# Layer 1 of a graph network: the table of ready halves written in steps of three chunks and read from the third gathered block on

## The chip, the core and the metric

The kernel runs on one core of one Trainium2 chip. The metric is the device time of one execution in microseconds (us); lower is better. The engines are named as in the profile: PE (TensorE, matrix products), DVE (VectorE), ACT (ScalarE), POOL (GpSimd, which issues the gathers) and SP (SyncE, which issues most other DMAs). PEld and SPq are PE's weight loads and SP's queue.

## What is computed

A graph network of three layers over 6250 nodes with 256 features and 100,000 edges that are sorted by destination, then a residual and a layer norm. Cut to what matters:

```python
loops = arange(n)
src, dst = concat([edges[0], loops]), concat([edges[1], loops])
deg = segment_sum(ones, dst);  dinv = rsqrt(deg)
h = x
for W, b in ((W1, b1), (W2, b2), (W3, b3)):      # 256->512, 512->512, 512->256
    msg = (h @ W)[src] * (dinv[src] * dinv[dst])[:, None]
    h = relu(segment_sum(msg, dst) + b)
out = layernorm(x + h)
```

The kernel sums over the edges before it multiplies by W1 (both are linear), so layer 1 sums rows of `dinv * x`, 256 numbers each.

## The kernel before

**Blocks and chunks.** The nodes are cut into 50 blocks of 125 (`NB`, `Q`). Each block has a run of 2048 places for edges, that is 16 chunks (`KF`) of 128 edges. Edges beyond these are gathered for ten blocks at once (`GRP`).

**Two ways to sum a block.** A *gathered* block takes its 16 chunks one after the other. POOL gathers the 128 source rows of a chunk by an indirect DMA (L1179), DVE makes one-hot matrices of the destinations (`shot`, L1130), and PE multiplies the one-hot matrix with the rows and adds up in a PSUM bank (L1209). A *dense* block instead uses a matrix of edge counts between its nodes and all nodes. Such counts are made on the chip (`counts`: one-hots of small windows of edges by DVE at L791, products at L866, copies out of PSUM by ACT at L825), stored to DRAM (`kept`, L818), converted by ACT (`piece`, L1139), and multiplied with `parts` (L1278).

**Halves.** `parts` holds `dinv * x` in SBUF, each row as a high half and a low half of 256 columns in the format fp32r. One product with 512 columns sums both halves. Layer 1 has three ways to get a gathered row:

- blocks before `BOTH_FROM` gather plain rows of 256 fp32 numbers from `tables[0]` (128 x 1 KB per chunk) into one of eight row buffers (`rows`). Their product is an fp32 matmul with 256 columns, which the trace records as two instructions of 256 columns. The block's own row (the self loop) is one more product with an identity matrix (L1192).
- blocks from `BOTH_FROM` to 47 gather rows of 512 ready halves from the DRAM table `both_halves` (in the profile `both`; 128 x 2 KB per chunk) into one of eleven buffers (`split`). Their product is one fp32r matmul with 512 columns. The block's own row is added by DVE (L1314) after the sum.
- blocks 48 and 49 (`TAIL_FROM`) gather plain rows and split them on ACT and DVE (L1241, L1244).

**The table of halves.** `both_stored` (L1499) writes `parts` to the table by ten stores of five blocks, 125 x 5 rows of 2 KB or 1.28 MB each. `by_rows` (L73) makes two DMAs of every store, of 112 and of 13 partitions. The generator yields 5 after each store: it continues five chunks later. A gather from the table names the whole table as its input, so the first one waits for all ten stores.

**The order of the work.** `layer` (L1048) writes all engines' queues out by hand, chunk by chunk. For layer 1 the gathered blocks are 22 to 49, so item 0 is the gather for the group of ten, items 1 to 16 are block 22, items 17 to 32 block 23, items 33 to 48 block 24, items 49 to 64 block 25 and items 65 to 80 block 26. In each chunk come the gather of that item, the product of the item five chunks back (`BOTH_LAG`), the steps that follow an ended block (`after1`: scaling, transposes at L1299, the product with W1 at L1335, the store of the result to `tab1`), then the fixed extras (`both_stored` starts at chunk 2; the counts and the searches for windows, which end in a gather at L521, start at 0), and at the end up to three dense products. Each engine works through its own queue in order; SP's queue holds the stores of the table, those of the counts (`kept<-room`) and those of the results (`tab<-st`). In the program's order the first two counted blocks are stored in chunks 18 and 31.

**A room that is lent.** When the first six chunks of block `BOTH_FROM` have been issued (L1164), a part of the row buffers becomes a third buffer for the one-hots of the counts (`late_hot_room`).

Of the kernel before, what the change touches and what calls it, by code (L numbers as in the profile page):

```python
# [47 lines left out]


FEW = 22  # L50
BOTH_FROM = 26
BOTH_LAG = 5
TAIL_FROM = 48
TAIL_LAG = 7
# [18 lines left out]
def by_rows(queue, tile_rows, dram_rows, store=False):  # L73

    for s in (slice(0, EVEN), slice(EVEN, Q)):
        if store:
            queue.dma_start(out=dram_rows[s], in_=tile_rows[s])  # L77
        else:
            queue.dma_start(out=tile_rows[s], in_=dram_rows[s])
# [320 lines left out]
def sorted_path(ctx: ExitStack, tc: tile.TileContext, x, edges, starts, found, wts, biases, room, late, out):  # L400
# [647 lines left out]
    def layer(i, width, gathered, dense, after, rows, first=0, spacing=1.0, extras=(), filler=None):  # L1048
# [53 lines left out]
        def sum_bank(name, most):  # L1102
            nonlocal late
            if i == 0:
                while not common:
                    if early_copy[0]():
                        break
                    late += 1
                    go(chunk)
                return common.popleft()  # L1110
            need(now, name, most)
            return idle[name].pop(0)
# [33 lines left out]
        def of_both(c):  # L1146

            n, b, _ = items[c]
            return i == 0 and (n * GRP >= BOTH_FROM if b is None else BOTH_FROM <= b < TAIL_FROM)

# [9 lines left out]
        def gather(c):  # L1160
            nonlocal turn
            n, b, j = items[c]
            table = both_halves if of_both(c) else tables[i]
            if (i, b, j) == (0, BOTH_FROM, BOTH_LAG + 1):  # L1164
                hot_stores.appendleft(late_hot_room)
# [16 lines left out]
        def product(c):  # L1182
# [4 lines left out]
            if j == 0:  # L1187
                acc = sum_bank("acc", 2 if i == 1 else 3)
                own_product = i == 0 and b < BOTH_FROM
                if own_product:  # L1190
# [113 lines left out]
    def after1(b, acc, bank):  # L1304
        got = []
        yield from take("zs", 2)
        zs = work.tile([Q, HID], F32, name="szs")
        if b < BOTH_FROM:
            nc.scalar.activation(zs[:, :C], acc[:Q, C:], AF.Copy, scale=dinv[:, b:b + 1])
# [189 lines left out]
    def both_stored(first):  # L1499

        for b in (*range(first, NB, GRP // 2), *range(0, first, GRP // 2)):
            to = slice(b, b + GRP // 2)
            by_rows(nc.sync, parts[:, to].bitcast(F32),
                    both_halves[b * Q:(b + GRP // 2) * Q, :].rearrange("(b p) c -> p b c", p=Q), store=True)
            yield 5

    def steps(b):

# [12 lines left out]
    first = 16  # L1521
    spacing = 15.0
    layer(0, C, every[FEW:], few, after1, first_rows, first, spacing, [(0, other_parts()), (2, both_stored(2 * GRP)), (0, searches), (1, counts(many[:FEW + EXTRA], places, GB, True)), (0, team_work)])

    assert len(common) == 7 - len(team_banks)
# [209 lines left out]
```

## Time and profile before

| | |
|---|---|
| three runs | 2097.81, 2102.70 and 2103.22 us; median 2102.7 |
| the profiled execution | 2106.41 us, its span 2104.7 us, mean granted PE clock 0.958 |
| PE, DVE, POOL, ACT busy, share of the span | 92%, 75%, 69%, 64% |
| gathers of layer 1 | from 78.8 us on; the first from the table of halves at 182.9 us |
| DMA over the span | 494.26 MB, mean 235 GB/s |

The profile gives, for one execution, each engine's busy time, its instructions in order of time, and for an idle stretch what released the engine. The window view gives busy time, the granted PE clock (1.00 is full speed), the mean busy share of the 16 DMA engines and their rate for chosen stretches. A line such as `L1209 PE MATMUL smm<-room,shot` is an instruction by its line of the kernel, its engine, and what it writes and reads. In a timeline the columns are start, duration, engine, line, operation, names, shapes, count, and in brackets the idle time before it with its releaser.

### The profile page before, as it was taken

Reading aid. Unit: us, or ns where it says so; the run is one execution under the profiler, and the core shown is the slowest. Engines: PE = TensorE matmul, PEld = TensorE weight load, DVE = VectorE, ACT = ScalarE, POOL = GpSimd, SP = SyncE. Lnnn points to the kernel's source line nnn. Section 1 sums busy time; section 2 is a strip of 40 time slices with the busy share of each in tenths; the row PEclk is TensorE's granted clock in tenths of the full one; section 3 lists DMA queues with packets and bytes.
Section 4 is the critical chain, followed back from the end, with each engine's and each line's share of the span. In section 5 each row is a group of like instructions: output and inputs, shape, how many; then the busy total and the mean of one; then the engine's idle time right before and its main releaser. Section 6 shows DMA issues by size and latency. Waiting matters only on the chain. (4 is left out here: it accounts for less than half of the span.)

```text
span 2104.7 us, 30190 instructions
## 1 busy us (share of the span) xinstructions
PE 1946.5 (92%) x8645; PEld 1507.4 (72%) x8645; DVE 1570.6 (75%) x2963; ACT 1351.5 (64%) x2587; POOL 1442.0 (69%) x1442
## 2 busy tenths in 40 slices
PE   3499999999997988999999999999898899999996
PEld 2377777777774656888778877888676777777774
DVE  5876777787777578777877778787776377777777
ACT  0566777677776666767766767777565455555553
POOL 2466766776767477767766777667776477777775
PEclk6599999999999989999999999999998899999998
DMA  7887989999999999899997999999988376767674
GB/s 156 260 250 222 255 241 246 245 265 252 255 261 308 240 274 263 255 260 286 279 262 209 294 273 275 258 267 271 252 231 240 91 190 176 188 178 189 177 185 117
DMA packets 236333, 494.26 MB, mean 235 GB/s; under 512 B 43807, under 2 KB 86889, under 8 KB 236155
## 3 DMA queue, kind: packets, MB, share of 16 engines
q0 software_dynamic: 122112, 311.41, 53.7%
q1 hardware_dynamic: 98203, 168.96, 29.2%
q10 hardware_dynamic: 15840, 11.86, 2.3%
q8 instruction: 70, 1.15, 0.2%
q14 instruction: 108, 0.88, 0.1%
HBM read 424.61 MB, written 67.46 MB: 234 GB/s over the span
## 5 line engine op out<-in xcount | busy, mean ns | idle before, releaser
L1179 POOL DMA_INDIRECT room<-tab,ssrc x1040 | 1077.8, 1036 | 394.6 <-issue 164.5
L1244 DVE TENSOR_TENSOR halves<-room,halves 128x512 fp32r<-128x512 f32 (+1 forms) x776 | 424.1, 561 | 226.2 <-ACT halves L1241 223.8
L1241 ACT CAST halves<-room 128x512 fp32r<-128x512 f32 (+1 forms) x776 | 386.3, 517 | 222.5 <-DMA room<-tab,ssrc 192.6
L1209 PE MATMUL sacc<-halves,shot 128*125 128x512 f32 x1401 | 494.6, 418 | 31.0 <-DVE halves L1244 16.4
L1179 POOL DMA_INDIRECT halves<-both,ssrc x352 | 331.5, 942 | 142.9 <-issue 36.3
L1209 PEld LDWEIGHTS sacc<-halves,shot 128*125 128x125 f32 x1401 | 261.8, 191 | 120.8 <-DVE halves L1244 35.8
L1139 ACT CAST piece<-room 125x625 fp32r<-125x625 uint8 x416 | 294.5, 716 | 75.3 <-DVE halves L1244 21.9
L791 DVE TENSOR_TENSOR room<-near_cols,slots 128x625 bf16<-128x625 f32 (+2 forms) x390 | 294.2, 802 | 42.6 <-PE sacc L866 17.7
L1130 DVE TENSOR_TENSOR shot<-near_cols,sdlo 128x500 fp32r<-128x500 f32 x371 | 247.7, 668 | 6.4 <-PE smm L1209 3.7
L1278 PE MATMUL mat_ps<-parts,piece 125*125 125x512 f32 x650 | 187.0, 405 | 0.0
L1244 DVE TENSOR_TENSOR parts<-room,parts 128x512 fp32r<-128x512 f32 x200 | 136.3, 692 | 58.6 <-ACT parts L1241 57.9
L1278 PE MATMUL win_ps<-parts,piece 125*125 125x512 f32 x600 | 171.2, 406 | 4.9 <-ACT piece L1139 4.8
L1278 PE MATMUL smm<-parts,piece 125*125 125x512 f32 x605 | 171.8, 402 | 0.6 <-DVE piece L1139 0.6
L1241 ACT CAST parts<-room 128x512 fp32r<-128x512 f32 x200 | 121.8, 622 | 64.3 <-DMA room<-tab,ssrc 57.4
L939 DVE TENSOR_TENSOR parts<-parts 125x512 fp32r<-125x512 f32 x200 | 137.9, 690 | 32.2 <-ACT parts L937 29.4
L977 PE MATMUL sacc<-parts 125*125 125x512 f32 x400 | 143.7, 434 | 17.6 <-ACT parts L937 9.7
L825 ACT CAST room<-sacc 125x500 uint8<-125x500 f32 (+1 forms) x152 | 105.6, 703 | 71.9 <-PE sacc L866 56.8
L866 PEld LDWEIGHTS <-room 128*125 128x125 bf16 x650 | 89.5, 140 | 76.6 <-issue 29.6
L1278 PE MATMUL sacc<-parts,piece 125*125 125x512 f32 x450 | 142.2, 423 | 0.4 <-ACT piece L1139 0.4
L977 PE MATMUL mat_ps<-parts 125*125 125x512 f32 x400 | 137.6, 425 | 0.7 <-DVE room L1378 0.7
L1278 PEld LDWEIGHTS mat_ps<-parts,piece 125*125 125x125 f32 x650 | 116.7, 187 | 27.8 <-issue 2.3
L1278 PEld LDWEIGHTS win_ps<-parts,piece 125*125 125x125 f32 x600 | 111.3, 189 | 33.3 <-ACT piece L1139 5.8
(345 smaller groups left out, 3252.6 us busy)
## 6 DMA issues: line engine op xcount, KB each, us to landing
parts<-tab SPq DMA_DIRECT2D x105, 448.0 KB
kept<-room SPq DMA_DIRECT2D x29, 683.6 KB
room<-kept SPq DMA_DIRECT2D x29, 683.6 KB
room<-tab,ssrc POOLq DMA_INDIRECT x1040, 5.6
tab<-st SPq DMA_DIRECT2D x62, 224.0 KB
both<-parts SPq DMA_DIRECT2D x10, 1120.0 KB
own_row<-tab SPq DMA_DIRECT2D x38, 224.0 KB
parts<-kept SPq DMA_DIRECT2D x60, 136.7 KB
```

Of the source, the lines that this page charges most:

```text
L791: nc.vector.tensor_tensor(out, near_cols[:, :shape[2]].unsqueeze(1).to_broadcast(shape), numbers.unsqueeze(2).to_broadcast(shape), op=ALU. ...
L825: nc.scalar.copy(place[:, :, u * G:(u + len(ms)) * G].rearrange("p k (t r) -> p t k r", r=G), counted_in.rearrange("p (t v) -> p t v", t=2 ...
L866: nc.tensor.matmul(bank[:Q, len(pair) * 256:][:, :G * NB], lhsT=hot_lo, rhs=hot_key, start=True, stop=True)
L939: nc.vector.tensor_sub(to[:, HID:], row, to[:, :HID].bitcast(F32))
L977: nc.tensor.matmul(team_banks[n][:Q], lhsT=team_pieces[(g * CUTS + k // PIECE) % 2][n][:, k % PIECE, :], rhs=both_parts[u % 3][:, h * HID: ...
L1130: nc.vector.tensor_tensor(hot[:, :n], near_cols[:, :Q].unsqueeze(1).to_broadcast([P, n, Q]), dlo.rearrange("p b j -> p (b j)")[:, at:at + ...
L1139: convert(piece, made_or_read[:, c * PIECE:(c + 1) * PIECE, :])
L1179: nc.gpsimd.indirect_dma_start(out=row, out_offset=None, in_=table, in_offset=bass.IndirectOffsetOnAxis(ap=at, axis=0))
L1209: nc.tensor.matmul(acc[:Q, :size], lhsT=hot, rhs=row[:, c0:c0 + size], start=(not own_product and k == c0 == 0), stop=(k == KF and c0 + si ...
L1241: nc.scalar.copy(halves[:, :width], landed[chunk - hi_lag])
L1244: nc.vector.tensor_sub(halves[:, width:], landed.pop(chunk - lo_lag), halves[:, :width].bitcast(F32))
L1278: nc.tensor.matmul(acc_d[:Q], lhsT=got[done // PIECE][:, k % PIECE, :], rhs=parts[:, k], start=(k == 0), stop=(k == NB - 1))
```

## The change

`both_stored` continues three chunks after each store, not five: the ten stores are issued in chunks 2, 5, 8, ..., 29, not 2, 7, 12, ..., 47. `BOTH_FROM` becomes 24, not 26: blocks 24 and 25 (items 33 to 64) gather ready halves from the table instead of plain rows, have no own product at L1192 and get their own row by L1314; the room for one-hots is lent at chunk 39, not 71.

```diff
 FEW = 22
-BOTH_FROM = 26
+BOTH_FROM = 24
 BOTH_LAG = 5
...
             by_rows(nc.sync, parts[:, to].bitcast(F32),
                     both_halves[b * Q:(b + GRP // 2) * Q, :].rearrange("(b p) c -> p b c", p=Q), store=True)
-            yield 5
+            yield 3
```

## Prediction

> **What bounds the kernel now.** I read the windows of layer 1's start first, then the timelines of PE, SP and POOL, the waits of PE, and the list of DMA issues. The span of the profiled execution is
>
> ```profile
> span 2104.7 us, 30190 instructions
> ```
>
> and its time 2106.41 us: 1.7 us lie around the span, and it is 3.7 us (0.18%) above the median of 2102.7 us. I work with differences in the profiled execution and carry them over to the median. About 0.3%, or 6.3 us, is what a measurement of this kernel can tell from no change.
>
> The windows (length, busy time of PE, PEld, DVE, ACT, POOL, granted clock, DMA share, rate):
>
> ```profile
> 78.00:84.00 6.00, 0.00 (x0) 0.00 (x0) 6.00 (x4) 1.95 (x1) 4.92 (x2) 0.50 0.47 131
> 84.00:102.00 18.00, 8.11 (x29) 6.05 (x30) 15.94 (x22) 3.94 (x7) 12.30 (x10) 0.54 1.00 310
> 102.00:114.00 12.00, 9.60 (x38) 7.07 (x37) 11.72 (x22) 5.80 (x9) 9.20 (x10) 0.72 0.55 170
> 114.00:138.00 24.00, 21.94 (x111) 17.05 (x110) 16.74 (x26) 17.51 (x30) 15.15 (x17) 1.00 0.81 245
> 138.00:162.00 24.00, 24.00 (x120) 18.71 (x119) 17.19 (x32) 17.15 (x31) 15.92 (x18) 1.00 0.98 311
> 162.00:180.00 18.00, 18.00 (x83) 13.18 (x81) 10.48 (x20) 10.31 (x20) 10.17 (x11) 1.00 0.51 163
> 180.00:200.00 20.00, 20.00 (x95) 14.91 (x94) 13.07 (x27) 12.24 (x21) 13.95 (x16) 1.00 0.85 227
> ```
>
> From 138 us on PE has no idle time at all, at full clock: there PE is the bound, and every matmul time that goes is gained. Before that, PE is idle for parts of the time. The DMA engines are full in two stretches (share 1.00 and 0.98), and both times they move 310 to 311 GB/s: I take 0.31 MB/us as what they can do with this mix. Between, from 102 to 138, they have room.
>
> SP's queue shows where the stores stand:
>
> ```profile
> 81.51 16.19 SPq L77 DMA_DIRECT2D both<-parts  x8
> 114.17 0.76 SPq L77 DMA_DIRECT2D kept<-room  x2
> 114.97 5.78 SPq L77 DMA_DIRECT2D both<-parts  x4
> 134.97 0.77 SPq L77 DMA_DIRECT2D kept<-room  x2
> 135.79 10.73 SPq L77 DMA_DIRECT2D both<-parts  x6
> ```
>
> Four stores (two DMAs each) are issued as fast as SP gets them through. Then SP stands at the store of the first counted block until its counts are ready at 114.17, passes two more stores, stands again until 134.97, and passes three more; the tenth comes after a third such store. So the schedule in chunks matters little by itself: what counts is on which side of a counted block a store stands.
>
> **The matmuls: what is gained.** One chunk on PE with plain rows, one with ready halves, and an own product:
>
> ```profile
> 133.71 0.60 PE L1209 MATMUL win_ps<-room,shot 128*125 128x256 f32 x2
> 134.14 0.38 PE L866 MATMUL sacc<-room 128*125 128x250 bf16 x2
> 134.28 0.95 PE L1278 MATMUL sacc<-parts,piece 125*125 125x512 f32 x3
> 135.06 0.60 PE L1209 MATMUL win_ps<-room,shot 128*125 128x256 f32 x2
> ```
>
> ```profile
> 199.52 0.39 PE L1209 MATMUL smm<-halves,shot 128*125 128x512 f32 x1
> 199.76 0.38 PE L866 MATMUL sacc<-room 128*125 128x250 bf16 x2
> 199.89 0.94 PE L1278 MATMUL sacc<-parts,piece 125*125 125x512 f32 x3
> 200.67 0.39 PE L1209 MATMUL smm<-halves,shot 128*125 128x512 f32 x1
> ```
>
> ```profile
> 144.44 0.39 PE L1192 MATMUL smm<-parts,ident_r 125*125 125x512 f32 x1
> 144.67 0.60 PE L1209 MATMUL smm<-room,shot 128*125 128x256 f32 x2
> ```
>
> From start to start the product takes 134.14 - 133.71 = 0.43 us with plain rows and 199.76 - 199.52 = 0.24 with halves, and the whole chunk 1.35 and 1.15. That is 0.19 us for each of the 32 chunks of blocks 24 and 25, or 6.1 us. The two own products go too, 144.67 - 144.44 = 0.23 us each: 0.5. Together 6.5 us less work on PE, all of it after 144 us, where PE is never idle.
>
> Three things go along and I cost them at nothing. For two blocks DVE adds 512 columns (L1314) before ACT's scaling; DVE is busy for 13.07 us of the 20 from 180 to 200 and has room. The room for one-hots is lent 32 chunks earlier, which only lets DVE run further ahead. And POOL's issue of a gather costs the same from either table (0.94 us, rows below).
>
> **The table must be there: what is given back.** POOL's rows, first and 34th gather of the layer, and the first from the table:
>
> ```profile
> 78.77 3.19 POOL L1179 DMA_INDIRECT room<-tab,rest  x1 [13.76 <-DVE parts L676]
> ...
> 133.22 0.94 POOL L1179 DMA_INDIRECT room<-tab,ssrc  x1 [1.44 <-PE smm L866]
> ...
> 182.91 0.96 POOL L1179 DMA_INDIRECT halves<-both,ssrc  x1 [0.30 <-DMA tab<-st]
> 184.17 0.95 POOL L1179 DMA_INDIRECT halves<-both,ssrc  x1 [0.30 <-issue]
> ```
>
> Counted from item 0 at 78.77, the row at 133.22 is item 33, the first chunk of block 24. Before, it reads the plain table. The first gather from `both` comes at 182.91 with no more idle time before it than any other (0.30): the last store had long landed. After the change item 33 itself waits for all ten stores, and its product is due when PE comes to block 24, at 144.4.
>
> When can the stores have landed? Six of them, of chunks 2 to 17, now stand before the first counted block in SP's queue, and four (20, 23, 26, 29) behind it and before the second. From 84 us on the DMA engines always have something to do. The sizes and landing times:
>
> ```profile
> both<-parts SPq DMA_DIRECT2D x10, 1120.0 KB
> ...
> halves<-both,ssrc POOLq DMA_INDIRECT x352, 4.7
> ```
>
> With the 13 partitions of the second DMA a store is 1.28 MB. What has to move before the last has landed: ten stores, 12.8 MB; 33 gathers of 128 x 1 KB, 4.3 MB; one counted block, 125 x 6250 bytes, 0.8 MB; and weights and bias that the code loads at that time, 0.8 MB. Together 18.7 MB. Of these 0.8 MB move from 78 to 84 (131 GB/s in the window). The other 17.9 MB take 17.9 / 0.31 = 57.7 us, so the last store lands at about 142 us; with the rate of 114 to 138 scaled to a full share (245 / 0.81 = 302 GB/s) at 143. POOL, ready at 133, stands for 9 us with all later gathers behind it. Item 33 is then issued at 142.3 and lands after 4.7 us, the median, at 147.0: 2.6 us after PE wants it. If it landed as slowly as gathers do beside stores,
>
> ```profile
> DMA to landing us min/median/max: 9.2/9.2/9.2
> ```
>
> (those issued from 122 to 128, behind two stores and a counted block), it would be 151.5, or 7.1 us late. Behind the last store SP has only the second counted block, so I stay near the first: 3.2 us. Should gathers come late before that, PE reaches block 24 later by as much and waits there the less: the bytes are the same, and the two do not add up.
>
> The Trainium skill's page HBM Reference (Specifications) says that a core which streams alone measures about 425 GB/s. With that figure the stores would have landed at 126 and nothing would be given back; both full stretches of this trace stay at 310 and 311, and the measurement decides.
>
> **What follows the stall.** POOL starts without a lead. It issues a gather every 184.17 - 182.91 = 1.26 us, and PE needs 1.15 for a bare chunk with halves: up to 0.1 us a chunk for 16 chunks, 1.6 us, until the products of an ended block (L1335) let POOL get ahead. I take 0.7. The gather at L521 stands four places behind item 33 and is held with it; DVE meets its result only after item 37's product, which is held too: nothing extra. The clock can fall. After the waits of 102 to 109 us it did:
>
> ```profile
> 112.04 1.06 PE L1209 MATMUL smm<-room,shot 128*125 128x256 f32 x2
> 112.90 0.41 PE L866 MATMUL win_ps<-room 128*125 128x250 bf16 x1
> ```
>
> There the product takes 0.86 us against 0.43 at full clock. Bounds: nothing, or some 4 us at half clock, which cost 2. I take 1.0. The page TensorE: Matmul & The Clock Gate of the Trainium skill (Part 1) has the clock halve after an idle window of about 3.4 us and come back after as long a busy one: for a single stall of 3.2 us that gives 0 or 1.7 us, and the window of 102 to 114, at 0.72 after shorter waits, shows that less idle time can be enough.
>
> **The sum:** -6.5 + 3.2 + 0.7 + 1.0 = -1.6 us. All later work is placed by chunks and keeps its order, so the difference stays to the end: 2104.8 us for the profiled execution, about 2101 for the median.
>
> **Rivals.**
>
> *The DMA engines keep up* (chance 0.28). A chunk's gathers may come later than before, or the rate may be higher than 0.31, and the table may land by 137; then the whole 6.5 us stay: 2096.2 us. For it: 102 to 114 has half of the DMA engines' time free, and 0.34 MB/us would do (17.9 MB in the 53 us to 137). Against it: both full stretches say 310.
>
> *PE is starved on the way* (0.15). With ten stores back to back, the gathers of plain rows land late all the way from 102 to 142. Each wait is short, but the clock does not hold. What PE waited for there before:
>
> ```profile
> PE smm L1209 <- DMA both<-parts: 3.2, 1, 3.2
> PE smm L1209 <- DMA room<-tab,ssrc: 2.4, 3, 1.1
> PE win_ps L1209 <- DMA room<-tab,ssrc: 1.7, 2, 1.1
> ```
>
> That is 7.3 us with six stores; with ten, in proportion, 12.2, so 4.9 more. If the 28 us from 114 to 142 ran at the clock of 0.72 of the stretch before, they would take 10.9 us longer. PE then comes to block 24 after the table has landed, and the stall of 3.2 is gone. Between 10.9 - 6.5 = +4 and +9 us: about 2109. It decides if waits and lost clock before block 24 come to over 13 us. Against it: from 138 to 162 the DMA engines were just as full beside plain gathers, and PE was never idle.
>
> *The change moves the bound to POOL* (0.10). If blocks 24 and 25 run at POOL's 1.26 us a chunk rather than PE's pace, it saves only 0.09 x 32 + 0.5 = 3.4 us, and the stall takes 3.2 of it: 2102.5. For it: the two paces above. Against it: a block's other products (L1335, L1299) make PE the slower one over 16 chunks.
>
> **How the numbers follow.** The forecast has a chance of 0.47. It lies within 0.3%, as does the POOL rival; the first rival sits on the edge of it (6.5 against 6.3), and a good half of its chance counts as faster, with a little from the forecast: 0.20. Slower is nearly all of the starved case: 0.15. The rest, 0.65, is the same. The range goes from the whole gain with the spread of a median of few runs, 2094.5, to the middle of the starved case, 2108.5.
>
> **What would show it.** In the profile after: gathers from `both` from item 33 on, POOL idle for several us before the first and released by a store to `both`; that gather landing near 147; one idle stretch of PE of 2 to 5 us before the first product of block 24, which no own product precedes; a DMA share near 1 from 84 to 142; the first product of block 26 about 2 us earlier than before, where it is
>
> ```profile
> 196.79 0.40 PE L1209 MATMUL smm<-halves,shot 128*125 128x512 f32 x1
> ```
>
> I am wrong if POOL does not wait there, if PE's waits before block 24 are much over 7 us, or if the gain at block 26 is not there at the end.

## The result, and the profile after

| | before | after |
|---|---|---|
| median of 20 runs | 2102.09 us | 2106.06 us |
| lowest to highest | 2090.49 to 2111.03 | 2101.23 to 2123.71 |
| ratio | | 1.0038, 95% interval 1.0022 to 1.0054 |
| profiled execution, its span | 2106.41, 2104.7 us | 2101.23, 2099.6 us |

The changed kernel is slower, by 0.38% or 8 us (0.0038 of 2102; the interval is 4.6 to 11.3 us). The ratio compares runs taken side by side; the two medians alone lie 4.0 us apart, the means of the 20 runs 6.4 us. The forecast was no measurable change, with 1.6 us less as its value. The profiled execution of the changed kernel has the shorter span all the same. A single span tells nothing here: three profiles of the kernel before have spans of 2104.7, 2101.5 and 2094.1 us. So I compare the profiles stage by stage. After block 26 of layer 1 has begun, both kernels run the same instructions in the same order, and what one of them is late by at that point is the measure of the change.

The windows of the profile after, the same stretches as before:

```profile
78.00:84.00 6.00, 0.00 (x0) 0.00 (x0) 5.77 (x7) 0.00 (x0) 5.08 (x4) 1.00 0.75 248
84.00:102.00 18.00, 10.07 (x39) 7.20 (x39) 16.70 (x26) 6.33 (x10) 13.15 (x11) 1.00 1.00 301
102.00:114.00 12.00, 8.17 (x26) 5.93 (x27) 7.79 (x13) 3.46 (x6) 6.93 (x8) 0.57 0.91 291
114.00:138.00 24.00, 22.15 (x116) 17.61 (x114) 17.40 (x27) 19.01 (x33) 11.01 (x12) 1.00 0.97 301
138.00:162.00 24.00, 19.38 (x82) 14.14 (x81) 13.96 (x28) 12.85 (x23) 12.95 (x14) 0.86 0.69 189
162.00:180.00 18.00, 15.46 (x63) 11.01 (x62) 10.69 (x20) 9.63 (x17) 13.73 (x15) 0.91 0.94 257
180.00:200.00 20.00, 20.00 (x94) 14.58 (x93) 14.62 (x29) 12.83 (x22) 15.06 (x17) 1.00 0.98 275
```

The DMA engines are full or nearly so from 84 to 138 (shares of 0.91 to 1.00), as foreseen. (The clock of 1.00 from 84 to 102 is no gain over the 0.54 of before; the section on the kernel before, again, says why.) From 138 to 180, where PE was never idle in the first profile before, it is now idle for 4.6 + 2.5 us, and for part of the rest it runs at half clock (0.86 and 0.91 in the mean). SP's queue and POOL's:

```profile
78.45 27.42 SPq L77 DMA_DIRECT2D both<-parts  x12
114.46 0.80 SPq L77 DMA_DIRECT2D kept<-room  x2
115.31 17.27 SPq L77 DMA_DIRECT2D both<-parts  x8
133.05 4.17 SPq L77 DMA_DIRECT2D kept<-room  x2
```

```profile
130.12 0.95 POOL L1179 DMA_INDIRECT room<-tab,ssrc  x1 [0.30 <-PE mat_ps L866]
145.09 0.95 POOL L1179 DMA_INDIRECT halves<-both,ssrc  x1 [14.02 <-DMA both<-parts]
146.35 0.95 POOL L1179 DMA_INDIRECT halves<-both,ssrc  x1 [0.30 <-issue]
```

With two issues to a store, six stores go ahead of the first counted block (x12) and four behind it (x8), and POOL stands for 14.02 us before the first gather from the table, released by a store. On PE the same place, and a second one eleven chunks later:

```profile
143.01 0.95 PE L1278 MATMUL sacc<-parts,piece 125*125 125x512 f32 x3
148.58 0.76 PE L1209 MATMUL smm<-halves,shot 128*125 128x512 f32 x1 [4.62 <-DMA halves<-both,ssrc]
149.14 1.91 PE L1335 MATMUL mat_ps<-w,room 128*125 128x512 f32 x2
150.06 2.27 PE L1278 MATMUL sacc<-parts,piece 125*125 125x512 f32 x3
...
164.22 0.94 PE L1278 MATMUL sacc<-parts,piece 125*125 125x512 f32 x3
167.70 0.50 PE L1209 MATMUL smm<-halves,shot 128*125 128x512 f32 x1 [2.54 <-DMA halves<-both,ssrc]
```

The three dense products at 150.06 take 2.27 us, those at 143.01 took 0.95: half clock behind the wait. Block 26 begins at

```profile
201.21 0.40 PE L1209 MATMUL smm<-halves,shot 128*125 128x512 f32 x1
```

against 196.79 in the first profile before. The two executions did not begin this stage at the same time: SP issues the first store at 81.51 us in the profile before and at 78.45 here, and block 22 begins 10.5 us behind the first store in both, at 92.04 and 88.97. Counted from the start of block 22, block 26 begins after 104.75 us before and after 112.24 us now: it is 7.5 us late.

### The profile page after: what moved, and what is told of

It reads as the page before. It is cut to its first block, busy times and chain, and to the rows that moved or that the text cites. A ratio compares the mean times of both kernels' runs of the same rounds, so it can differ in the third digit from the quotient of the medians.

```text
span 2099.6 us, 30122 instructions
## 1 busy us (share of the span) xinstructions
PE 1934.7 (92%) x8611; PEld 1493.1 (71%) x8611; DVE 1572.3 (75%) x2965; ACT 1350.6 (64%) x2587; POOL 1434.7 (68%) x1442
## 3 DMA queue, kind: packets, MB, share of 16 engines
q0 software_dynamic: 125184, 315.61, 54.5%
## 4 chain that ended last, share of the span: by engine, by line
PE 31%; DMA 13%; issue 9%; DVE 8%; POOL 5%; ACT 3%; ACTq 0%; DVEq 0%; POOLq 0%
DMA room<-tab,ssrc 12%; PE sacc L1209 9%; POOL room L1179 5%; PE win_ps L1417 4%; PE win_ps L1278 3%; DVE halves L1244 3%; PE sacc L977 2%; PE mat_ps L977 2%; PE smm L977 2%; PE smm L1278 2%; PE win_ps L1437 2%; PE mat_ps L1278 2%; ACT halves L1241 1%; DVE shot L1130 1%; PE str L1417 1%
## 5 line engine op out<-in xcount | busy, mean ns | idle before, releaser
L1179 POOL DMA_INDIRECT room<-tab,ssrc x1008 | 1040.8, 1033 | 374.6 <-issue 161.2
L1179 POOL DMA_INDIRECT halves<-both,ssrc x384 | 361.2, 941 | 166.3 <-issue 40.0
L1278 PE MATMUL smm<-parts,piece 125*125 125x512 f32 x605 | 171.7, 402 | 0.6 <-DVE piece L1139 0.6
L939 DVE TENSOR_TENSOR parts<-parts 125x512 fp32r<-125x512 f32 x200 | 138.0, 690 | 28.5 <-ACT parts L937 24.6
L1278 PEld LDWEIGHTS win_ps<-parts,piece 125*125 125x125 f32 x600 | 111.3, 189 | 32.9 <-ACT piece L1139 5.5
```

The source lines that it names most:

```text
L939: nc.vector.tensor_sub(to[:, HID:], row, to[:, :HID].bitcast(F32))
L1179: nc.gpsimd.indirect_dma_start(out=row, out_offset=None, in_=table, in_offset=bass.IndirectOffsetOnAxis(ap=at, axis=0))
L1278: nc.tensor.matmul(acc_d[:Q], lhsT=got[done // PIECE][:, k % PIECE, :], rhs=parts[:, k], start=(k == 0), stop=(k == NB - 1))
```

## The experiments

The theory after the result, called *landing*: the bytes on the DMA engines hold the tenth store back to 145 us, POOL stands for it, and the wait on PE and what follows it cost more than the 6.5 us saved. Rivals: *starved* (ten stores back to back slow the plain gathers and the clock before block 24), *SP's queue* (the stand at the first counted block holds the stores back, not the bytes), *clock* and *no lead* (what follows the wait).

The number that I read from every profile is when PE begins a block: its first product, or the own product ahead of it. Block 22 begins 10.5 us behind the first store in all fourteen profiles, so the column "22 to 26" leaves out how early an execution reached layer 1. All in us:

| kernel | block 22 | block 24 | block 25 | block 26 | 22 to 26 | ratio of times, 95% interval |
|---|---|---|---|---|---|---|
| before, first profile | 92.04 | 144.44 | 169.23 | 196.79 | 104.75 | |
| before, second | 89.79 | 139.70 | 165.94 | 193.50 | 103.71 | 0.9972, 0.9943 to 1.0002 |
| before, third | 88.31 | 140.67 | 165.45 | 193.01 | 104.70 | 1.0009, 0.9978 to 1.0041 |
| changed | 88.97 | 148.58 | 177.04 | 201.21 | 112.24 | 1.0038, 1.0022 to 1.0054 |
| changed, second | 88.51 | 147.85 | 175.56 | 199.76 | 111.25 | 1.0011, 0.9990 to 1.0033 |
| changed, two apart | 89.03 | 147.99 | 176.25 | 200.42 | 111.39 | 1.0039, 1.0013 to 1.0064 |
| changed, wait filled | 89.03 | 149.34 | 176.41 | 200.60 | 111.57 | 1.0016, 0.9992 to 1.0040 |
| spacing alone | 89.74 | 142.25 | 167.00 | 194.56 | 104.82 | 1.0007, 0.9986 to 1.0028 |
| spacing alone, second | 88.73 | 144.24 | 168.80 | 196.36 | 107.63 | 1.0019, 0.9993 to 1.0045 |
| one apart, from block 26 | 89.64 | 143.35 | 168.39 | 195.95 | 106.31 | 1.0003, 0.9975 to 1.0031 |
| the wait alone | 89.18 | 141.07 | 172.90 | 200.46 | 111.28 | 1.0030, 1.0003 to 1.0057 |
| from block 25 | 89.15 | 144.72 | 169.29 | 193.47 | 104.32 | 0.9982, 0.9954 to 1.0010 |
| from block 25, second | 89.82 | 149.37 | 173.93 | 198.12 | 108.30 | 1.0007, 0.9978 to 1.0036 |
| from block 25, four apart | 89.34 | 146.62 | 171.18 | 195.37 | 106.03 | 0.9991, 0.9967 to 1.0014 |

The two repeats of the kernel before show what the times can tell: 0.3% one way or the other is within one such comparison. The block starts are steadier, and the times follow them: the five kernels that take 111 us or more from block 22 to block 26 have ratios with a mean of 1.0027, the other eight (the repeats of before among them, 103.7 to 108.3 us) 0.9999.

**The kernel before, again.**

```diff
(no edit)
```

> The kernel before, once more: what two sets of runs of one program differ by (ratio 1 within 0.2%), and a second profile, whose first stretch may have another granted clock than the 0.54 from 84 to 102 us that the first had. First product of block 26 between 194 and 197 us.

> The kernel before, a third profile. From the first product of block 22 to that of block 24 it took 52.4 us in the first profile and 49.9 in the second. Theory 'both' (the denser stores also slow blocks 22 and 23, besides the wait for the table): 50 to 52.5 again, under the 55 of most kernels with the stores three apart. Theory 'landing alone': anything from 50 to 56, the stretch being a matter of chance in either kernel.

Block 26 began at 193.50 and 193.01, just under the foreseen 194 to 197, and the ratio of the second set, 0.9972, lies a little outside the foreseen 0.2%. Blocks 22 and 23 together took 49.9 and 52.4 us; in the first profile it was 52.4. The second profile's start of block 24 and of block 26:

```profile
139.70 0.39 PE L1192 MATMUL smm<-parts,ident_r 125*125 125x512 f32 x1
```

```profile
193.50 0.40 PE L1209 MATMUL smm<-halves,shot 128*125 128x512 f32 x1
```

These starts are 4.7 and 3.3 us earlier than in the first profile. At first sight the clock explains that: the window view gives 1.00 from 84 to 102 us in the second and third profile, and 0.54 in the first. The products in that stretch say otherwise. First the first profile, then the second:

```profile
95.99 1.19 PE L1209 MATMUL smm<-room,shot 128*125 128x256 f32 x2 [3.18 <-DMA both<-parts]
99.01 1.06 PE L1209 MATMUL smm<-room,shot 128*125 128x256 f32 x2
101.08 0.59 PE L1209 MATMUL smm<-room,shot 128*125 128x256 f32 x2
```

```profile
93.81 1.19 PE L1209 MATMUL smm<-room,shot 128*125 128x256 f32 x2 [3.25 <-DMA both<-parts]
96.83 1.06 PE L1209 MATMUL smm<-room,shot 128*125 128x256 f32 x2
98.97 0.59 PE L1209 MATMUL smm<-room,shot 128*125 128x256 f32 x2
```

It is the same sequence, 2.2 us earlier: a pair of instructions takes 1.06 to 1.19 us, as at half clock, and then 0.59. The traces of the second and third profile have no clock record ahead of 98.5 us, and the view counts a stretch without a record as full clock. So the start was no faster in them. All of layer 1 was earlier: item 0 was gathered at 76.38 and 74.93 us instead of 78.77, the first store issued at 79.26 and 77.78 instead of 81.51, and block 22 begun at 89.79 and 88.31 instead of 92.04. Counted from block 22, block 24 was due after 52.4 us in the first profile, 49.9 in the second and 52.4 in the third.

On that count the changed kernel begins block 26 after 112.24 us, against 104.75, 103.71 and 104.70 before (mean 104.39): 7.9 us late, which is the size that the ratio gives.

**The changed kernel, again.**

```diff
(no edit)
```

> The changed kernel itself on the same chip as the others. Theory 'landing': slower than before by 4.3 us (what its block 26 was late in the profile) to 8 us (what the repeated timings gave); a wait of POOL of over 10 us before item 33, a wait of PE of about 4.6 us at the first product of block 24 and one of about 2.5 us inside the block.

POOL's first gather from the table came at 144.34 after 13.47 us of idle time, PE waited 4.80 us at block 24's first product and 0.42 + 1.41 + 1.24 inside the block, and block 26 began at 199.76. So the picture of the first profile repeats, with the second wait split into smaller ones; counted from block 22, block 26 is 6.9 us late (111.25 against the mean of 104.39). The times of this set show less than that: a ratio of 1.0011 is 2 us, under the foreseen 4.3 to 8, and its interval includes no change.

**The spacing alone.**

```diff
-BOTH_FROM = 24
+BOTH_FROM = 26
```

> Stores three chunks apart, but the table is read from block 26 on as before (item 65). Theory 'landing' (the loss is the wait of block 24's first gather for the tenth store, which the bytes on the DMA engines hold back to 145 us, and what follows that wait): nothing waits for the table here, no change from before, within 2 us; no idle of POOL before the first gather from the table; PE waits before 144 us no more than 2 us longer than before. Rival 'starved' (ten stores back to back slow the plain gathers and the clock): slower than before by 4 us or more, with long waits of PE for plain gathers between 102 and 142.

> The spacing alone, a second profile (52.5 us for blocks 22 and 23 in the first). Theory 'both': 52 to 60 us, like the others with this spacing. Theory 'landing alone': like the kernel before, 50 to 52.5.

No gather waited for the table (0.30 us of idle time before the first one, at 180.68 and 182.49). Counted from block 22, block 26 began after 104.8 and 107.6 us, which is 0.4 and 3.2 us behind the mean of the three profiles before. The times (1.0007 and 1.0019) cannot tell that from nothing. Blocks 22 and 23 took 52.5 us in the first of the two, as before, and 55.5 in the second, and there the whole difference lies.

**The early cost, made larger.**

```diff
-BOTH_FROM = 24
+BOTH_FROM = 26
-            yield 3
+            yield 1
```

> The suspected early cost made larger: the stores one chunk apart (chunks 2 to 11, all ten ahead of the first counted block), the table read from block 26 on, so that nothing waits for it. Theory 'both': blocks 22 and 23 take 56 us or more, PE waits over 10 us in all for plain gathers before block 24, and block 26 starts that much later than in the kernel before. Theory 'landing alone': 50 to 53 us, and block 26 within 1 us of the kernel before.

Blocks 22 and 23 took 53.7 us, between the two expectations, PE waited 8.0 us for plain gathers, under the 10 of theory 'both', and block 26 began 1.9 us later than the mean before, counted from block 22. More stores ahead of the first counted block did not cost more than six of them. The windows from 102 to 114 say what the kernels share, first this one, then the second profile before:

```profile
102.00:114.00 12.00, 7.65 (x30) 5.23 (x31) 8.03 (x17) 3.91 (x6) 7.21 (x8) 0.86 1.00 311
```

```profile
102.00:114.00 12.00, 8.27 (x36) 6.27 (x37) 10.75 (x20) 6.19 (x10) 8.95 (x11) 0.86 0.57 165
```

Before, four stores have gone by 102 us and the DMA engines are at 0.57: the gathers of block 22 come through. With five or more stores ahead of the counted block they are busy at 0.70 to 1.00 in this stretch. In the kernels with denser stores, blocks 22 and 23 take 51.9 to 57.3 us up to block 24's start where no wait for the table counts in (with one outlier of 59.6; 55.0 in the changed kernel, up to its wait), before 49.9 to 52.4. The mean with denser stores is some 3 us larger, but the two ranges overlap, it scatters as much as it is large, and more stores ahead did not cost more. That the denser stores cause this early cost is likely, and not shown.

**Does SP's queue hold the stores back?**

```diff
-            yield 3
+            yield 2
```

> The changed kernel with the stores two chunks apart: nine instead of six stand before the first counted block's store in SP's queue, so they need not wait for its counts. Theory 'landing' (the bytes set the time of the tenth store, the DMA engines being full from 84 to 138 us already): the first gather from the table still comes at 142 to 146 us, and the time is that of the changed kernel within 2 us. Rival 'SP's queue' (the stand at the first counted block is what holds the last stores back): the first gather comes at 138 us or earlier and 4 us or more of the loss are gone.

```profile
78.50 46.46 SPq L77 DMA_DIRECT2D both<-parts  x18
125.06 4.53 SPq L77 DMA_DIRECT2D kept<-room  x2
```

```profile
144.53 0.96 POOL L1179 DMA_INDIRECT halves<-both,ssrc  x1 [12.58 <-DMA kept<-room]
145.79 0.94 POOL L1179 DMA_INDIRECT halves<-both,ssrc  x1 [0.31 <-issue]
```

With nine stores ahead of the first counted block (x18), SP never stands for its counts: it is still issuing stores when they come, up to 125. (The releaser that the profile names here is the store of the second counted block, as in the second profile of the changed kernel, while the first profile names a store to the table. The landings in the traces settle it: the last landing of the tenth store is at 144.16, 143.41 and 143.59 us in the two profiles of the changed kernel and in this one, and POOL's gather starts 0.93 or 0.94 us behind it in all three, while the last landings of the counted block come after the gather has started. So it is the tenth store that POOL waits for.) The first gather from the table comes at 144.53, against 145.09 and 144.34. The tenth store lands no sooner when SP issues nearly all of them early: what the DMA engines have to move sets the landing, and the rival falls. Block 26 at 200.42 and the ratio of 1.0039 are those of the changed kernel.

**The wait without the gain.**

```diff
-BOTH_FROM = 24
+BOTH_FROM = 26
...
+            if (i, b, j) == (0, 24, 0):
+                nc.gpsimd.dma_start(out=own_pool.tile([1, 16], F32, name="looked"), in_=both_halves[15 * Q:15 * Q + 1, :16])
             nc.gpsimd.indirect_dma_start(out=row, out_offset=None, in_=table,
```

> Stores three apart, table read from block 26 on as before; but ahead of block 24's first gather (of plain rows) POOL reads 64 bytes of the last stored rows of the table, so it stands until the tenth store has landed, and blocks 24 and 25 keep their plain rows. The wait without the gain. Theory 'landing': POOL stands until about 145, block 24's first product comes near 151, and block 26 is late by the wait of PE plus the half clock behind it, 6 to 10 us against the kernel with the spacing alone, since POOL's 1.25 us is under PE's 1.35 a chunk with plain rows and the lead comes back. If the loss is larger than that only where 2 KB rows are gathered (theory 'no lead': in the changed kernel the work of 6.5 us was saved and block 26 was still 4.3 to 6.5 late, so its wait cost 11 to 13), there are no second waits here.

```profile
141.89 0.55 POOL L1180 DMA_DIRECT2D looked<-both  x1 [12.25 <-DMA both<-parts]
142.75 1.00 POOL L1181 DMA_INDIRECT room<-tab,ssrc  x1 [0.30 <-issue]
```

```profile
141.07 0.40 PE L1194 MATMUL smm<-parts,ident_r 125*125 125x512 f32 x1
145.56 1.22 PE L1211 MATMUL smm<-room,shot 128*125 128x256 f32 x2 [4.10 <-DMA room<-tab,ssrc]
```

POOL stood for 12.25 us, PE for 4.10, and there was no other wait on PE up to 200 us. Both stands ended earlier than foreseen: POOL's at 141.89 and not 145, PE's at 145.56 and not 151. Block 24 took 172.90 - 141.07 = 31.8 us, against 24.8 and 24.6 with the spacing alone: some 7.1 us for the wait, of which 4.1 are the wait itself and 3.0 the half clock behind it (the product at 145.56 takes 1.22 us). That is within the 6 to 10 expected. Block 26, 111.3 us behind block 22, is as late as in the changed kernel, without its gain.

**The wait filled with work.**

```diff
                 own_product = i == 0 and b < BOTH_FROM
+                if i == 0 and b == BOTH_FROM:
+                    for _ in range(16):
+                        nc.tensor.matmul(acc[:Q], lhsT=ident_r[:Q, :Q], rhs=parts[:, b], start=True, stop=True)
```

> The changed kernel with 16 more products into block 24's bank ahead of its first product (overwritten by it, so the result is unchanged): 16 x 0.23 = 3.7 us of work that fits into PE's wait of 4.6 us and keeps the clock up. Theory 'landing' with its clock part (the wait of 4.6 us costs another 2.5 because PE runs at half clock until 154 us): about 2.5 us faster than the changed kernel, the chunks of block 24 at full clock from 148.6 on, though the second wait inside block 24 may grow since PE gets to it earlier: 0 to 2.5 us faster. If the clock does not matter: 3.7 us or so later only if the gather lands earlier than 147.5, else the same time as the changed kernel.

```profile
145.63 3.87 PE L1192 MATMUL smm<-parts,ident_r 125*125 125x512 f32 x16
149.34 0.39 PE L1212 MATMUL smm<-halves,shot 128*125 128x512 f32 x1
```

```profile
PE smm L1212 <- DMA halves<-both,ssrc: 4.6, 5, 1.7
```

The sixteen products fill the time up to the landing, the clock stays at 1.00 through block 24, and yet block 26 begins 111.6 us behind block 22, as in the changed kernel (112.2 and 111.3). What the clock no longer costs, PE now waits for gathers inside block 24: five times, 4.6 us in all. So the clock is not the limit there, the gathers are. In the changed kernel, from 160 to 172, with the item whose product waited at 167.70 issued at 160.42:

```profile
160.00:172.00 12.00, 9.46 (x41) 7.11 (x40) 8.31 (x16) 6.37 (x12) 8.95 (x11) 0.86 1.02 290
```

The DMA engines are full again (1.02): POOL issues gathers of 256 KB without a pause after its stand, beside the third counted block and a result. That gather took 167.7 - 160.4 = 7.3 us to land rather than 4.7, and with no lead PE meets every such delay.

**Reading from block 25 on.**

```diff
-BOTH_FROM = 24
+BOTH_FROM = 25
```

> Stores three chunks apart, table read from block 25 on (item 49). Theory 'landing': item 49 is issued near 153 us, well after the tenth store has landed at about 145; no wait, and the one block's 16 x 0.19 + 0.23 = 3.3 us are gained: about 3 us faster than before (2 to 4), 7 faster than the changed kernel. Rival 'lead' (gathers of 2 KB rows in this stretch cannot be fed whatever the table does: POOL's 1.25 us a chunk against PE's 1.15): PE waits again inside block 25, at most 1 us gained. Rival 'starved': slower than before.

> The version that reads from block 25 on, once more: 2 to 4 us faster than before, with no wait of POOL for the table.

```profile
157.41 0.95 POOL L1179 DMA_INDIRECT halves<-both,ssrc  x1 [0.37 <-issue]
```

The first gather from the table, at 157.41 and 162.06, waits for nothing, and PE does not wait inside block 25. Block 25 takes 24.18 and 24.19 us instead of 27.56: 3.4 us are gained, and theory *no lead* does not hold where POOL has its lead. But blocks 22 and 23 took 55.6 and 59.6 us, so block 26 began 104.3 and 108.3 us behind block 22, and the times of the two sets (0.9982 and 1.0007) are those of no change.

```diff
-BOTH_FROM = 24
+BOTH_FROM = 25
-            yield 3
+            yield 4
```

> Table read from block 25 on, stores four chunks apart (2 to 38). Both theories: block 25 is 3.4 us shorter. Theory 'both': blocks 22 and 23 take 50 to 54 us, less than with three apart, and the first gather from the table (due near 153) waits for at most 3 us, since POOL has about 5 us of lead there: 1 to 3 us faster than before. If the tenth store, behind the second counted block now, lands after 158, PE waits at block 25 and nothing is gained.

No wait for the table either (0.37 us before the first gather, at 159.31), block 25 again 3.4 us shorter, but blocks 22 and 23 took 57.3 us, more than expected, with PE waits of 8.7 + 2.8 us for plain gathers. The time is that of no change (0.9991). No version was found that beats the kernel before beyond the interval.

## Why the prediction was wrong

**Right:** the mechanism that I gave as the likeliest. POOL stands before item 33 until the tenth store has landed, issuing the stores earlier does not bring that forward, PE stands at block 24's first product, and half clock follows.

**Right:** the gain. Block 25 is 27.56 - 24.18 = 3.4 us shorter in every kernel that reads it from the table; I had 3.3 for each block.

**The step that failed first: "The other 17.9 MB take 17.9 / 0.31 = 57.7 us".** The forecast for item 33, 142.3 us, looks close to the measured 145.1, 144.3, 144.5 and 145.5, but that is luck: it was worked out on the times of the one profile that began this stage late. Counted from the start of block 22, the forecast is 142.3 - 92.04 = 50.3 us and the measured times are 56.1, 55.8, 55.5 and 56.5. My 57.7 us began at 84.00, which is 2.49 us behind the first store. In the changed profile the same point is 80.94, and the tenth store's last landing is at 144.16: that took 63.2 us.

```profile
80.94:141.00 60.06, 43.39 (x194) 33.20 (x195) 46.52 (x71) 31.18 (x52) 33.54 (x32) 0.91 0.97 303
141.00:144.16 3.16, 2.96 (x13) 1.77 (x11) 3.16 (x6) 2.48 (x5) 0.00 (x0) 1.00 0.33 118
```

By these two rows 18.6 MB moved, 0.7 more than I had counted: the store of the second counted block, 0.8 MB, which I had put behind the tenth store, landed beside it (its landings run from 137.4 to 146.1 us). At 0.31 MB/us that is 2.3 us. The other 3.2 us are the rate: 303 GB/s and not 310 up to 141 us, and then a tail in which the DMA engines were busy for a third of the time. All landings but one of the tenth store's two DMAs are recorded by 141.61 and 142.09 us; the last one of each comes at 143.75 and 144.16. Why these come 2 us behind the others is open.

The first gather then landed in 3.5 us (145.09 to 148.58) and not in the median of 4.7, which by chance gave 1.2 us back. So block 24's first gathered product came 59.6 us behind block 22's start, where the forecast has 147.0 - 92.04 = 55.0 and the three profiles before 52.6, 50.1 and 52.6. The term of 3.2 us should have been 7 to 9.5, or 7.8 in the mean. The due time, "at 144.4", held in one of the two repeats and was 2.5 us earlier in the other; that is what a single profile left open.

**The step that failed second: "what follows the stall", 0.7 + 1.0.** Block 24 with halves, from its first product on, should have taken 24.8 - 3.3 + 1.7 = 23.2 us. It took 28.5, 27.7 and 28.3: about 5 us more. The clock alone was under-priced: I had 1.0 us for it, from half of some 4 us at half clock. In the changed profile half clock lasted 6.8 us (147.8 to 154.6), and the first three chunks took 7.0 us (148.58 to 155.58) where the filled wait, at full clock, took 4.1 (149.34 to 153.44). But at full clock block 24 still took 176.41 - 149.34 = 27.1 us. Behind a stand the gathers have no lead, POOL issues them back to back, the DMA engines fill, and a landing of 7.3 us instead of the median of 4.7 stops PE once more, which in the first changed profile lowers the clock once more. I had priced POOL's pace and the clock for one wait each, and neither is the limit by itself, as the filled wait shows.

With both terms as measured the sum closes: -6.7 saved (3.3 foreseen in block 24, 3.4 measured in block 25), +7.8 at block 24's first product, +1.7 and +5 inside block 24. That makes 7.8 us, against 7.9 and 6.9 at block 26 in the two profiles of the changed kernel.

**The rivals.** *The DMA engines keep up* did not happen: 291 to 301 GB/s at shares of 0.91 to 1.00 up to 138 us. *Starved* happened in part: PE's waits for plain gathers before block 24 are 9.1 and 8.3 us in the two profiles of the changed kernel against 7.3, 5.2 and 4.9 in the three before, and PE reached its wait for the table 55.0 and 54.5 us behind block 22's start instead of 49.9 to 52.4. Its stall did not go away and its 10.9 us of lost clock did not come. In the changed kernel this is hidden, as I had said, since block 24 waits for the table anyway. But where nothing waits for the table some 3 us of it show, and use up the gain of reading from block 25. *POOL as the bound* named one part of the restart: no more than that, since it had the loss end at 2102.5.

The range and the chances leaned on a small net difference between terms of 3 to 7 us each. The first of them is itself the difference of a transfer of 58 us and a due time, and an error of a tenth in that transfer was enough to turn the sign.

## What to carry to other kernels

Before you compare times of two executions, count both from an event ahead of the change: here the start of block 22, which removes a shift of up to 3.7 us that has nothing to do with either kernel. When the end of a bulk transfer sets a stall, price what lands beside it and its tail, and not only the bytes ahead of it at the full rate. Check a granted clock of 1.00 against the length of one product in the same stretch before you explain anything by it. When a producer's queue stands for longer than its lead, price the restart as a stretch without lead, where each landing above the median is a new wait, and not as one wait. And look at where a bulk write's pause used to be before you bring it forward: here the DMA engines were half idle in it, and the first block's gathers may have needed that.

## What the runs showed of the hardware

In all three profiles before, PE runs at half clock when block 22 begins and reaches full clock 8.6 to 10.3 us later: at 100.6, 98.5 and 98.6 us, by the clock records and by the length of the products, 1.06 us and then 0.59.

A wait of 2.54 us was enough to bring half clock: in the changed kernel the three dense products behind it took

```profile
168.18 1.52 PE L1278 MATMUL sacc<-parts,piece 125*125 125x512 f32 x3
```

against 0.94 before it. The Trainium skill, page TensorE: Matmul & The Clock Gate (Part 1), gives an idle window of about 3.4 us for this. The wait here is shorter, and the trace, which has half clock from 168.3 to 171.7 us, decides; one execution with waits of 1.41 and 1.24 us in the same place (the changed kernel's second profile) kept 1.00 from 162 to 180.
